# Transposing y by a copy through DRAM and by blocks on VectorE, in a kernel of 32 steps on one core

## The chip, the cores and the metric

The kernel runs on one core of a Trainium2 chip. The metric is device time in microseconds; the smaller, the better. All arithmetic that matters here is in float32. A core has a TensorE (matrix products, PE in the profile), a VectorE (DVE), a ScalarE (ACT), a GpSimd (POOL) and a SyncE (SP), which in this kernel issues most of the DMAs. Each engine works through its own instructions in order, and so does each queue of DMA issues; engines meet through semaphores.

## The reference

Two blocks follow each other, each with a residual sum and a layer norm behind it. The first is a layer that is trained on each token while it runs, the second a mixture of experts:

```python
def step(carry, kvq):                      # per sequence, 4096 tokens in order
    W, b = carry
    k, v, q = kvq                          # projections of the token, width 512
    pred = W @ k + b
    g = 2.0 / d_h * (pred - v)
    W = W - LR * jnp.outer(g, k)
    b = b - LR * g
    return (W, b), W @ q + b
...
x = layernorm(x + attn(x))                 # x: 2 sequences x 4096 tokens x 512
...
shared = silu(X @ sW1 + sb1) @ sW2 + sb2
logits = X @ routing_W + expert_bias       # 8 experts, the best 2 are used
activation = sqrt(softplus(logits))
routed = sum over the 2 best e of activation_e * (silu(X @ rW1_e + rb1_e) @ rW2_e + rb2_e)
x = layernorm(x + shared + routed)
```

The hidden width of each expert is 256.

## The kernel before

**Steps.** The 4096 tokens are cut into 32 chunks of 128, and one step of the loop, `step(c)`, treats chunk c of both sequences (B = 2). Inside a chunk the recurrence is solved as a triangular system. What a step needs of the inputs is made a step ahead: `prep(c + 1)` makes the keys and queries (tile KQ; PE tile pkq) and their products with each other (pa); `invert(c)` inverts the 32x32 blocks on the diagonal on VectorE, by 46 short instructions (line 375, tile X). Their result goes to DRAM and back (dX, CT; lines 382 and 384) and is then masked (C, D, DT, M; lines 388 to 397) for `join(c)`, which makes the inverse of the whole block (pn, pz). `step(c)` makes the residual R (pr, with theta_V and W; line 442), the output (po), the solved errors (pe) and the update of W (pw; line 494). The bias of W is kept up by an all-reduce on GpSimd (line 483) and two additions (line 485), followed there by x+brep (line 443).

**The second block, one step later.** `shared(c - 1)`, run in step c, takes the normalized y of the chunk before. It transposes y on TensorE into the tile pt (line 607), ScalarE copies pt to yT (line 609), and yT is then the stationary operand of the first product (ph, line 621), which gives the hidden layer of the shared expert and the router's logits. `router` picks two experts for each token, counts places (pq) and scatters the token's code into a table (gt, line 588; the index ri, line 585). y itself goes to DRAM (gy, line 613), y plus the second bias (line 630) plus the shared expert's output (py) too (gb, line 673).

**Experts.** Chunks 0 to 22 are one group, 23 to 30 another. When a group is complete, `routed` gathers its tokens expert by expert, and `collect` adds the two expert rows of each token to gb, takes the mean and the variance and writes the normalized rows. For group 0 the routed part runs in steps 24 to 27, collecting from step 28 on. Chunk 31 goes through all eight experts in `dense`, at the end, beside the collecting of group 1. `collect` finishes two chunks at a time (`finish`: one square root on ScalarE for both, then the scaling and the write).

**Order.** The order of TensorE and VectorE is written out: each part of a step is a generator that emits instructions and yields an amount, and `interleave` always continues the part of which the smallest share has been done. The share is the amount yielded so far over the total that the caller names for the part: 44 for a step, 13.5 for `prep`, 95 for `invert` and 13.5 for `shared`. The other engines and queues (ScalarE, GpSimd, SP) are ordered by the scheduler. A step's order on TensorE and VectorE follows from these numbers alone.

**A transpose without TensorE is already there, for K.** In steps 1 to 23 the keys are transposed in two moves. `exchange` writes the tile to DRAM in four DMAs (dT, line 304), one for each group of 32 columns, and reads it back in four others (G, line 307), so that quarters of partitions and quarters of columns change places; `turn_blocks` then transposes all 32x32 blocks in a single instruction of VectorE (line 315). The exchange of K is issued at the end of `prep(c + 1)`; its block transpose stands in the middle of the next step.

Of the kernel before, what the change touches and what calls it, by code (L numbers as in the profile page):

```python
# [41 lines left out]
F32 = mybir.dt.float32  # L42
BF16 = mybir.dt.bfloat16
I32 = mybir.dt.int32
AF = mybir.ActivationFunctionType
ALU = mybir.AluOpType
# [8 lines left out]
K = 2  # L55
# [5 lines left out]

SUMS = 23

TURNED = range(1, 24)
PSUM = bass.MemoryType.PSUM


# [39 lines left out]
def postln_block(ctx: ExitStack, tc: tile.TileContext, x, xT, thK, thV, thQ, w0, b0, masks, blk,  # L107
# [209 lines left out]
                                                                      a=NB, z=SB))  # L317


    prepared, turned = {}, {}  # L320

    def prep(c):
# [189 lines left out]
    def router(c, lg):  # L512
        def small(tag, shape=(P, B, E), bufs=1):
            return sm.tile(list(shape), F32, tag=tag, name=f"{tag}_{c}", bufs=bufs)


        u = small("u")
        nc.vector.scalar_tensor_tensor(u, lg, -1.0, lg, ALU.mult, ALU.min)
        nc.scalar.activation(u, u, AF.Exp)
        yield  # L520
        w = small("w")
        nc.vector.tensor_scalar(w, u, 1.0, None, ALU.add)
        lnw = small("lnw")
        nc.scalar.activation(lnw, w, AF.Ln)

        rank = small("rank")
        full = [P, B, E, E]
        other = lg[:, :, None, :].broadcast_to(full)
        own = lg[:, :, :, None].broadcast_to(full)
        gt = small("gt", full)  # L530
        nc.vector.tensor_tensor(gt, other, own, ALU.is_gt)
        eq = small("eq", full)
        nc.vector.tensor_tensor(eq, other, own, ALU.is_equal)
        nc.vector.tensor_tensor(eq, eq, lower[:, None].broadcast_to(full), ALU.mult)
        nc.vector.tensor_tensor(gt, gt, eq, ALU.add)
        nc.vector.tensor_reduce(rank, gt, AX.X, ALU.add)
        yield
        wm = small("wm")
        nc.vector.tensor_scalar(wm, w, -1.0, None, ALU.add)
        z = small("z")  # L540
        nc.vector.tensor_scalar(z, wm, 0.0, None, ALU.is_equal)
        nc.vector.tensor_tensor(lnw, lnw, z, ALU.add)
        nc.vector.tensor_tensor(wm, wm, z, ALU.add)
        nc.vector.reciprocal(wm, wm)
        nc.vector.tensor_tensor(lnw, lnw, wm, ALU.mult)
        nc.vector.tensor_tensor(lnw, lnw, u, ALU.mult)
        act = small("act")
        nc.vector.scalar_tensor_tensor(act, lg, 0.0, lnw, ALU.max, ALU.add)
        nc.scalar.activation(act, act, AF.Sqrt)
        if c not in of_step:  # L550

            nc.vector.scalar_tensor_tensor(act, rank, K - 0.5, act, ALU.is_lt, ALU.mult)
            yield act
            return

        gr = of_step[c]
        j = c - gr.c0
        chosen = sm.tile([P, B, E], BF16, tag="chosen", name=f"chosen_{c}")
        nc.vector.tensor_scalar(chosen, rank, K - 0.5, None, ALU.is_lt)
        sel = small("sel", (P, B, K, E))  # L560
        full = [P, B, K, E]
        nc.vector.tensor_tensor(sel, rank[:, :, None, :].broadcast_to(full),
                                kk[:, None, :, :].broadcast_to(full), ALU.is_equal)
        yield

        ps = ps_f.tile([P, 2, B, E], F32, tag="pf", name=f"pq_{c}")
        for s in range(B):
            nc.tensor.matmul(ps[:, 0, s], before, chosen[:, s], start=True, stop=(s == 0))
            for r in range(s):
                nc.tensor.matmul(ps[:, 0, s], ones16, chosen[:, r], start=False,  # L570
                                 stop=(r == s - 1))
        for s in range(B):
            nc.tensor.matmul(ps[:, 1, 0], ones16, chosen[:, s], start=(s == 0),
                             stop=(s == B - 1))
        yield
        place = small("place")
        nc.vector.tensor_tensor(place, ps[:, 0],
                                gr.next[:, None, :].broadcast_to([P, B, E]), ALU.add)
        nc.vector.tensor_tensor(gr.next, ps[:, 1, 0], gr.next, ALU.add)
        for what, to in ((place, gr.row), (act, gr.cw)):  # L580
            v = small("selv", (P, B, K, E))
            nc.vector.tensor_tensor(v, sel, what[:, :, None, :].broadcast_to(full), ALU.mult)
            nc.vector.tensor_reduce(to[:, j], v, AX.X, ALU.add)
        ri = sm.tile([P, B, K], I32, tag="ri", name=f"ri_{c}")
        nc.vector.tensor_copy(ri, gr.row[:, j])  # L585
        for s in range(B):
            for k in range(K):
                nc.gpsimd.indirect_dma_start(  # L588
                    out=gr.tables[s * K + k],
                    out_offset=bass.IndirectOffsetOnAxis(ap=ri[:, s, k:k + 1], axis=0),  # L590
                    in_=code[:, j * B + s:j * B + s + 1], in_offset=None,
                    bounds_check=E * gr.cap - 1, oob_is_err=False)

    def shared(c):
# [4 lines left out]
        y, norm = normed.pop(c)  # L599
        next(norm)  # L600
        yield 1.0
        yT = ytp.tile([P, DC, B, P], F32, tag="yT", name=f"yT_{c}")
        for dc in range(0, DC, 2):
            ps = ps_f.tile([P, 2, B, P], F32, tag="pf", name=f"pt_{c}_{dc}")
            for s in range(B):
                for i in range(2):
                    nc.tensor.transpose(ps[:, i, s, :], y[:, s, (dc + i) * P:(dc + i + 1) * P],
                                        ident)
            nc.scalar.copy(yT[:, dc:dc + 2].rearrange("p i s t -> p (i s t)"),
                           ps.rearrange("p i s t -> p (i s t)"))  # L610
        if gr:
            rows = slice((c - gr.c0) * T, (c - gr.c0 + 1) * T)
            nc.sync.dma_start(out=gr.y[rows].rearrange("(s p) d -> p s d", p=P), in_=y)
        yield 0.7

        lg = sm.tile([P, B, E], F32, tag="lg", name=f"lg_{c}")
        pre = hp.tile([P, B, HF + E], F32, tag="h", name=f"pre_{c}")
        for s in range(B):
            ps = ps_f.tile([P, HF + E], F32, tag="pf", name=f"ph_{c}_{s}")
            for dc in range(DC):  # L620
                nc.tensor.matmul(ps, yT[:, dc, s, :], w1_sb[:, dc, :],  # L621
                                 start=(dc == 0), stop=(dc == DC - 1))
            nc.scalar.copy(pre[:, s, :], ps)
            yield 1.5
# [68 lines left out]
    def dense(c):  # L693
# [4 lines left out]
        for e in range(E + 1):  # L698
            if e < E:
# [2 lines left out]
                    h = stepp.tile([P, 2, HC, T], F32, tag=("R", "K")[e // 2 % 2], name=f"hd_{e}", bufs=1)  # L702
                h_e[e] = h[:, e % 2]
                for hc in range(HC):
                    ps = ps_f.tile([P, T], F32, tag="pf", name=f"pd_{e}_{hc}")
                    for dc in range(DC):
                        nc.tensor.matmul(ps, w[:, dc * HF + hc * P:dc * HF + (hc + 1) * P],
                                         yT[:, dc].rearrange("p s t -> p (s t)"),
                                         start=(dc == 0), stop=(dc == DC - 1))
                    nc.scalar.activation(h_e[e][:, hc, :], ps, AF.Silu,  # L710
                                         bias=b1e_sb[:, e, hc:hc + 1])
                    yield 2.0
            if e > 0:
# [166 lines left out]
                weights(k + NW)  # L880
            yield 2.0

    squares, finish_at = [True], [(2, 3)]

    def collect(gr):

# [22 lines left out]
                    z.append(t)  # L909
                    yield  # L910

        def finish(parts, mean, var, on_scalar):

            if on_scalar:
                nc.vector.tensor_scalar(var, var, 1.0 / D, EPS, ALU.mult, ALU.add)
# [7 lines left out]
            for p, (c, acc) in enumerate(parts):  # L923
                for s in range(B):
                    m, v = mean[:, p, s:s + 1], var[:, p, s:s + 1]
                    if on_scalar:
                        nc.scalar.activation(acc[:, s, :], acc[:, s, :], AF.Identity,
                                             bias=m, scale=v)
                    else:
                        nc.vector.tensor_scalar(acc[:, s, :], acc[:, s, :], m, v,  # L930
                                                ALU.subtract, ALU.mult)
                nc.scalar.dma_start(out=out[:, c * P:(c + 1) * P, :].rearrange("s p d -> p s d"),
                                    in_=acc)
                yield

        for _ in fetch(0):
            pass
        yield 2.0
        done = iter(())
        for j in range(gr.n):  # L940
            c = gr.c0 + j
            ahead = fetch(j + 1)
            acc, z = got.pop(j)
            p = j % 2
            if p == 0:
                on_scalar, parts = squares[0], []
                two = sm.tile([P, 2, 2, B], F32, tag="fmv", name=f"fmv_{c}")
            mv = two[:, :, p]
            mean, var = mv[:, 0], mv[:, 1]
# [17 lines left out]
            else:  # L967
                for s in range(B):
                    st = sm.tile([P, 6], F32, tag="fst", name=f"fst_{c}_{s}")
                    nc.vector.bn_stats(st, acc[:, s, :])  # L970
                    nc.vector.bn_aggr(mv[:, :, s], st)
            if p == 1 or j == gr.n - 1:
                for _ in done:
                    pass
                done = finish(parts, two[:, 0, 0:p + 1], two[:, 1, 0:p + 1], on_scalar)
            yield 0.4
        for _ in done:
            pass
# [13 lines left out]
    for c in range(NCH):  # L992
# [3 lines left out]
        if c > 0:  # L996
            parts.append((INVERT, invert(c)))
        if c > 0:
            amount = SHARED + (PLAN if c in (b.c0, NCH - 1) else 0.0)
            parts.append((amount * (2 if c == NCH - 1 else 1), shared(c - 1)))  # L1000
        if c in spread:
            amount = (a.tiles + 3) * TILE / len(spread)
# [8 lines left out]
        if c == NCH - 2:  # L1011
            dense_weights(2)
    dense_weights(1 + B + 2)
    squares[0], finish_at[0] = False, (1, 3)
    interleave([(b.tiles * TILE, tiles[1]), (60.0, shared(NCH - 1)),
                ((a.n - sum(COLLECTED.values())) * COLLECT, collects[0])])
    squares[0] = True
    dense_weights(E - len(dense_w))
    interleave([(DENSE, dense(NCH - 1)), (b.n * COLLECT, collects[1])])


def _masks(np):
# [66 lines left out]
```

## Time and profile before

| What | Value |
|---|---|
| Median of 3 runs | 2638.32 us (2638.26 to 2647.33) |
| The profiled execution, its own time | 2633.89 us |
| Its span, first to last instruction | 2632.1 us |
| Mean granted TensorE clock | 0.989 |
| Length of each of the steps 1 to 22 | 58.66 us |
| VectorE idle before C (line 388), waiting for CT | 133.1 us in 27 waits |
| SP's dX waiting for the last instruction on X (line 382) | 364.6 us in 28 waits |
| Copies pt to yT on ScalarE | 64 of 128x512, 608 ns each |
| dT writes of K on SP | 92, median 680 ns of issue each, 128 KB |
| G reads of K on SP | 92, median 433 ns of issue each, 128 KB |

The span is cut into engines' busy times; an engine's idle time is put down to what ended it. The names are those of the tiles: `pt<-ident,x` is an instruction that writes the tile pt and reads ident and x (y lives in the tile x). The counts of matmul records are two for each float32 matmul of the program: `x8` at pkq is four matmuls, except for transposes, where eight records are eight transposes. Lines of SP's queue show the issue of a DMA, not its transfer.

### The profile page before, as it was taken

The numbers are of one execution on the slowest core, as the hardware profiler recorded it, in microseconds if no ns is written. First come the engines' busy times: TensorE is split into PE (matmuls) and PEld (weight loads), VectorE is DVE, ScalarE is ACT, GpSimd is POOL, SyncE is SP. The second block draws the span as 40 slices with busy tenths as digits, with TensorE's granted clock in tenths as the row PEclk, the third lists the DMA queues.
The fourth block names the chain that finished last, engine by engine and source line by source line (L and its number), as shares of the span: only waits on it lengthen the run. The fifth ranks groups of instructions, "written<-read, shape, count | busy, mean of one in ns | idle before, by whom it ended". The sixth has DMA issues, their size and how long they took to land.

```text
span 2632.1 us, 30914 instructions
## 1 busy us (share of the span) xinstructions
PE 2541.5 (97%) x10289; PEld 1642.1 (62%) x10289; DVE 1363.9 (52%) x3993; ACT 723.8 (27%) x1453; POOL 935.0 (36%) x796
## 2 busy tenths in 40 slices
PE   8999999999999999999999999999999999889897
PEld 6666666666666666666665676666767655446664
DVE  2566665565666655666666224223242466553345
ACT  1222222222222222222221232322323233334236
POOL 0223232223232322232324333333333334446654
PEclk9999999999999999999999999999999999989998
DMA  5122222222222222222223343353433456667777
GB/s 185 48 80 59 74 58 66 69 58 58 67 71 74 58 64 71 58 58 63 76 80 130 123 96 105 122 141 109 113 109 109 113 126 169 186 208 224 268 237 245
DMA packets 257647, 291.36 MB, mean 111 GB/s; under 512 B 158269, under 2 KB 171805, under 8 KB 253905
## 3 DMA queue, kind: packets, MB, share of 16 engines
q1 hardware_dynamic: 200624, 165.72, 22.1%
q0 software_dynamic: 48432, 107.42, 14.5%
q10 hardware_dynamic: 8432, 16.25, 1.6%
q8 instruction: 82, 1.34, 0.2%
q14 instruction: 77, 0.62, 0.1%
HBM read 344.38 MB, written 99.65 MB: 169 GB/s over the span
## 4 chain that ended last, share of the span: by engine, by line
PE 85%; issue 5%; DMA 4%; DVE 3%; POOL 2%; ACT 1%; SPq 0%; POOLq 0%; ACTq 0%; DVEq 0%
PE pkq L330 16%; PE pye L857 8%; PE po L449 8%; PE pr L433 8%; PE pr L438 8%; PE phe L846 8%; PE pw L493 8%; PE ph L621 4%; PE py L661 4%; PE pa L343 4%; PE pe L475 2%; PE po L487 2%; PE pg L837 2%; PE pz L414 2%; DMA wb<-wcat_in,widx 1%
## 5 line engine op out<-in xcount | busy, mean ns | idle before, releaser
L375 DVE SCALAR_TENSOR_TENSOR X<-L,X 128x31 f32<-128x31 f32 (+22 forms) x1472 | 409.0, 327 | 27.5 <-DMA L<-dL 10.5
L846 PEld LDWEIGHTS phe<-gT,wb 128*128 128x128 f32 x2208 | 269.7, 194 | 61.9 <-issue 58.9
L588 POOL DMA_INDIRECT gt<-code,ri x124 | 127.3, 1027 | 504.0 <-DVE ri L585 475.4
L860 DVE TENSOR_TENSOR o<-pye,wb 128x512 f32<-128x512 f32 x138 | 95.4, 692 | 400.8 <-PE pye L857 390.0
L857 PE MATMUL pye<-wb,he 128*128 128x512 f32 x552 | 268.7, 609 | 18.8 <-ACT he L850 11.9
L846 PE MATMUL phe<-gT,wb 128*128 128x128 f32 x2208 | 272.9, 277 | 7.0 <-DMA wb<-wcat_in,widx 5.6
L493 PE MATMUL pw<-R,K 128*128 128x512 f32 x496 | 240.6, 608 | 12.7 <-DVE x L488 7.9
L330 PE MATMUL pkq<-xT,thK 128*128 128x256 f32 x1024 | 242.8, 381 | 7.2 <-DMA thK<-thK_in 7.2
L828 POOL DMA_INDIRECT wb<-wcat_in,widx x138 | 144.8, 1049 | 286.2 <-DVE o L860 158.4
L330 PE MATMUL pkq<-xT,thQ 128*128 128x256 f32 x1024 | 244.9, 383 | 1.0 <-DVE Z L416 1.0
L330 PEld LDWEIGHTS pkq<-xT,thK 128*128 128x128 f32 x1024 | 195.0, 191 | 80.1 <-issue 59.3
L449 PE MATMUL po<-W,kq 128*128 128x512 f32 x512 | 242.6, 596 | 1.0 <-DVE K L471 1.0
L433 PE MATMUL pr<-thV,xT 128*128 128x512 f32 x512 | 240.7, 593 | 0.0
L438 PE MATMUL pr<-W,kq 128*128 128x512 f32 x512 | 240.2, 592 | 0.0
L330 PEld LDWEIGHTS pkq<-xT,thQ 128*128 128x128 f32 x1024 | 190.2, 191 | 46.9 <-issue 24.9
L483 POOL PARTITION_ALL_REDUCE ar<-R x23 | 141.6, 6158 | 206.4 <-issue 186.7
L850 ACT ACTIVATE he<-phe,wb 128x128 f32<-128x128 f32 x276 | 86.6, 364 | 436.5 <-PE phe L846 376.9
L337 ACT COPY kq<-pkq 128x256 f32<-128x256 f32 x256 | 82.8, 375 | 433.2 <-PE pkq L330 433.2
L494 DVE TENSOR_TENSOR W<-pw,W 128x512 f32<-128x512 f32 x248 | 168.5, 689 | 63.3 <-PE pw L493 59.6
L822 POOL DMA_INDIRECT g<-gy,gidx x138 | 139.8, 1013 | 153.4 <-PE pg L837 120.7
L493 PEld LDWEIGHTS pw<-R,K 128*128 128x128 f32 x496 | 91.4, 192 | 136.3 <-issue 97.8
L857 PEld LDWEIGHTS pye<-wb,he 128*128 128x128 f32 x552 | 98.5, 190 | 124.8 <-issue 90.8
(214 smaller groups left out, 3394.9 us busy)
## 6 DMA issues: line engine op xcount, KB each, us to landing
ge<-o SPq DMA_DIRECT2D x138, 256.0 KB
xT<-xT_in SPq DMA_DIRECT2D x32, 512.0 KB
x<-x_in SPq DMA_DIRECT2D x32, 512.0 KB
L<-dL SPq DMA_DIRECT2D x128, 128.0 KB
gy<-x SPq DMA_DIRECT2D x31, 512.0 KB
gb<-x SPq DMA_DIRECT2D x29, 512.0 KB
y_out<-acc ACTq DMA_DIRECT2D x29, 512.0 KB
dT_K<-kq SPq DMA_DIRECT2D x92, 128.0 KB
```

The costliest lines, as they stand in the source:

```text
L330: nc.tensor.matmul(ps[:, i].rearrange("p s t -> p (s t)"), th[:, dc, (ec + i) * P:(ec + i + 1) * P], xt[:, dc].rearrange("p s t -> p (s t) ...
L375: nc.vector.scalar_tensor_tensor(X[:, h, j + 1:], L[:, j + 1:, j], X[:, h, j:j + 1], X[:, h, j + 1:], ALU.mult, ALU.add)
L433: nc.tensor.matmul(ps, xt[:, dc, s, :], nthV_sb[:, dc, :], start=(dc == 0), stop=False)
L438: nc.tensor.matmul(ps, KQ[:, ec, s, 0, :], W[s][:, ec, :], start=False, stop=(ec == DC - 1))
L449: nc.tensor.matmul(ps, KQ[:, ec, s, 1, :], W[s][:, ec, :], start=(ec == 0), stop=False)
L483: nc.gpsimd.partition_all_reduce(ar, R, P, bass_isa.ReduceOp.add)
L493: nc.tensor.matmul(ps, K[s][:, ec, :], F[s], start=True, stop=True)
L494: nc.vector.tensor_tensor(W[s][:, ec, :], ps, W[s][:, ec, :], ALU.add)
L822: nc.gpsimd.indirect_dma_start(out=g_t[k], out_offset=None, in_=gr.y, in_offset=bass.IndirectOffsetOnAxis(ap=gr.gidx[:, k:k + 1], axis=0), ...
L828: nc.gpsimd.indirect_dma_start(out=wbuf[k % NW], out_offset=None, in_=wcat, in_offset=bass.IndirectOffsetOnAxis(ap=gr.widx[:, k:k + 1], ax ...
L846: nc.tensor.matmul(ps[:, hc, :], w[:, dc * HF + hc * P:dc * HF + (hc + 1) * P], t[:, dc, :], start=(dc == 0), stop=(dc == DC - 1))
L857: nc.tensor.matmul(ps, h[:, hc, :], w[:, O2 + hc * D:O2 + (hc + 1) * D], start=(hc == 0), stop=(hc == HC - 1))
```

## The change

In `shared(c)` for c = 1 to 21, which run in steps 2 to 22, the eight transposes on TensorE and the two copies on ScalarE are left out. y goes through `exchange` right after its write to gy is issued, then the generator yields `HELD` = 2.0, and `turn_blocks` writes yT. The total of `shared` grows by the same 2.0 in these steps, from 13.5 to 15.5. The tile yT has another layout, [P, B, DC, P] in place of [P, DC, B, P], in all steps, with the readers (ph, pd) and the copies that are left adapted to it. The copied tile G takes its buffer from the tag acc, which has four.

The instruction that makes `chosen` in `router` moves ahead by some ten instructions. In `collect` a chunk is finished alone where `paired[0]` is false (the part of group 0 that is collected in steps 28 to 31) and where it is one of a group's last two; else in pairs as before. For the last chunk of all, one sequence is scaled on VectorE and written through SP's queue, the other on ScalarE as before. The total that `interleave` is told for the collecting of group 1 is 1.1 times what it was.

```diff
@@ shared(c)
-        yT = ytp.tile([P, DC, B, P], F32, tag="yT", name=f"yT_{c}")
-        for dc in range(0, DC, 2):
-            ps = ps_f.tile([P, 2, B, P], F32, tag="pf", name=f"pt_{c}_{dc}")
-            for s in range(B):
-                for i in range(2):
-                    nc.tensor.transpose(ps[:, i, s, :], y[:, s, (dc + i) * P:(dc + i + 1) * P],
-                                        ident)
-            nc.scalar.copy(yT[:, dc:dc + 2].rearrange("p i s t -> p (i s t)"),
-                           ps.rearrange("p i s t -> p (i s t)"))
+        yT = ytp.tile([P, B, DC, P], F32, tag="yT", name=f"yT_{c}")
         if gr:
             rows = slice((c - gr.c0) * T, (c - gr.c0 + 1) * T)
             nc.sync.dma_start(out=gr.y[rows].rearrange("(s p) d -> p s d", p=P), in_=y)
+        if c in YTURNED:
+            g = exchange(y.rearrange("p s (c f) -> p (s c) f", f=P), f"y{c}")
+            yield HELD
+            turn_blocks(yT.rearrange("p s c t -> p (s c) t"), g)
+        for dc in range(0, DC, 2):
+            if c in YTURNED:
+                continue
+            ps = ps_f.tile([P, B, 2, P], F32, tag="pf", name=f"pt_{c}_{dc}")
...
         yield 0.7
@@ the readers of yT
-                nc.tensor.matmul(ps, yT[:, dc, s, :], w1_sb[:, dc, :],
+                nc.tensor.matmul(ps, yT[:, s, dc, :], w1_sb[:, dc, :],
...
-                                         yT[:, dc].rearrange("p s t -> p (s t)"),
+                                         yT[:, :, dc, :],
@@ collect
-            if p == 1 or j == gr.n - 1:
+            if p == 1 or not paired[0] or j >= gr.n - 2:
                 for _ in done:
                     pass
-                done = finish(parts, two[:, 0, 0:p + 1], two[:, 1, 0:p + 1], on_scalar)
+                done = finish(parts, two[:, 0, 0:p + 1], two[:, 1, 0:p + 1], on_scalar,
+                              gr is groups[-1] and j == gr.n - 1)
+                parts = []
@@ finish
-                    if on_scalar:
+                    if final and s == 0:
+
+                        nc.vector.tensor_scalar(acc[:, s, :], acc[:, s, :], v, m,
+                                                ALU.mult, ALU.add)
+                        nc.sync.dma_start(out=out[s, c * P:(c + 1) * P, :], in_=acc[:, s, :])
+                    elif on_scalar:
@@ the loop over steps and the end
-            amount = SHARED + (PLAN if c in (b.c0, NCH - 1) else 0.0)
+            amount = SHARED + (HELD if c - 1 in YTURNED else 0.0) + (PLAN if c in (b.c0, NCH - 1) else 0.0)
...
-    interleave([(DENSE, dense(NCH - 1)), (b.n * COLLECT, collects[1])])
+    interleave([(DENSE, dense(NCH - 1)), (1.1 * b.n * COLLECT, collects[1])])
```

with `HELD = 2.0` and `YTURNED = range(1, 22)`.

More of the change, by code (lines that the diff above doesn't have):

```diff
@@ L62 @@
 SUMS = 23
-TURNED = range(1, 24)
+TURNED, HELD = range(1, 24), 2.0
 PSUM = bass.MemoryType.PSUM
@@ L317, in turn_blocks @@
                                                                       a=NB, z=SB))
+    YTURNED = range(1, 22)
     prepared, turned = {}, {}
@@ L536, in router @@
         nc.vector.tensor_reduce(rank, gt, AX.X, ALU.add)
+        if c in of_step:
+            chosen = sm.tile([P, B, E], BF16, tag="chosen", name=f"chosen_{c}")
+            nc.vector.tensor_scalar(chosen, rank, K - 0.5, None, ALU.is_lt)
         yield
@@ L557, in router @@
         j = c - gr.c0
-        chosen = sm.tile([P, B, E], BF16, tag="chosen", name=f"chosen_{c}")
-        nc.vector.tensor_scalar(chosen, rank, K - 0.5, None, ALU.is_lt)
         sel = small("sel", (P, B, K, E))
@@ L613, in shared @@
             nc.sync.dma_start(out=gr.y[rows].rearrange("(s p) d -> p s d", p=P), in_=y)
+        if c in YTURNED:
[6 more added lines that the diff above has]
+            ps = ps_f.tile([P, B, 2, P], F32, tag="pf", name=f"pt_{c}_{dc}")
+            for s in range(B):
+                for i in range(2):
+                    nc.tensor.transpose(ps[:, s, i, :], y[:, s, (dc + i) * P:(dc + i + 1) * P],
+                                        ident)
+            nc.scalar.copy(yT[:, :, dc:dc + 2], ps)
         yield 0.7
@@ L704, in dense @@
                 for hc in range(HC):
-                    ps = ps_f.tile([P, T], F32, tag="pf", name=f"pd_{e}_{hc}")
+                    ps = ps_f.tile([P, B, P], F32, tag="pf", name=f"pd_{e}_{hc}")
                     for dc in range(DC):
                         nc.tensor.matmul(ps, w[:, dc * HF + hc * P:dc * HF + (hc + 1) * P],
-                                         yT[:, dc].rearrange("p s t -> p (s t)"),
+                                         yT[:, :, dc, :],
                                          start=(dc == 0), stop=(dc == DC - 1))
-                    nc.scalar.activation(h_e[e][:, hc, :], ps, AF.Silu,
+                    nc.scalar.activation(h_e[e][:, hc, :], ps.rearrange("p s t -> p (s t)"), AF.Silu,
                                          bias=b1e_sb[:, e, hc:hc + 1])
@@ L881, in routed @@
             yield 2.0
-    squares, finish_at = [True], [(2, 3)]
+    squares, finish_at, paired = [True], [(2, 3)], [False]
     def collect(gr):
@@ L910, in fetch, with finish @@
                     yield
-        def finish(parts, mean, var, on_scalar):
+        def finish(parts, mean, var, on_scalar, final):
             if on_scalar:
@@ L931, in finish @@
                                                 ALU.subtract, ALU.mult)
-                nc.scalar.dma_start(out=out[:, c * P:(c + 1) * P, :].rearrange("s p d -> p s d"),
-                                    in_=acc)
+                if final:
+                    nc.scalar.dma_start(out=out[1, c * P:(c + 1) * P, :], in_=acc[:, 1, :])
+                else:
+                    nc.scalar.dma_start(
+                        out=out[:, c * P:(c + 1) * P, :].rearrange("s p d -> p s d"), in_=acc)
                 yield
@@ L938, in collect @@
         yield 2.0
-        done = iter(())
+        done, parts = iter(()), []
         for j in range(gr.n):
@@ L943, in collect @@
             acc, z = got.pop(j)
-            p = j % 2
+            p = 0 if len(parts) != 1 else 1
             if p == 0:
-                on_scalar, parts = squares[0], []
+                on_scalar = squares[0]
                 two = sm.tile([P, 2, 2, B], F32, tag="fmv", name=f"fmv_{c}")
@@ L1013, in postln_block @@
     dense_weights(1 + B + 2)
-    squares[0], finish_at[0] = False, (1, 3)
+    squares[0], finish_at[0], paired[0] = False, (1, 3), True
     interleave([(b.tiles * TILE, tiles[1]), (60.0, shared(NCH - 1)),
```

## The prediction

> **What bounds it now.** I read the page's busy shares and its 40 slices, then one step of the loop engine by engine, because shares alone hide what waits inside a step.
>
> ```profile
> PE 2541.5 (97%) x10289; PEld 1642.1 (62%) x10289; DVE 1363.9 (52%) x3993; ACT 723.8 (27%) x1453; POOL 935.0 (36%) x796
> ```
>
> TensorE is busy nearly throughout. The step that begins at 843.92 us (c = 14), in the view by windows, is stricter: busy time equals length.
>
> ```profile
> 843.92:902.58 58.66, 58.66 (x210) 36.61 (x209) 35.14 (x108) 13.93 (x26) 17.61 (x13) 1.00 0.26 65
> ```
>
> Columns: window and length, then busy PE, PEld, DVE, ACT, POOL; clock, DMA share, GB/s. All of steps 1 to 22 last 58.66 us. So in the steps that the change touches each us off TensorE's order counts in full, and each us of wait put into it counts in full too. VectorE has 23 us to spare, but where? The timeline of VectorE at the head of the step:
>
> ```profile
> 848.41 7.18 DVE L375 SCALAR_TENSOR_TENSOR X<-L,X 128x29 f32<-128x29 f32 x36
> 857.16 0.69 DVE L442 TENSOR_TENSOR R<-pr,brep 128x512 f32<-128x512 f32 x1 [1.58 <-POOL brep L485]
> 857.77 5.87 DVE L375 SCALAR_TENSOR_TENSOR X<-L,X 128x4 f32<-128x4 f32 x8
> 868.26 0.24 DVE L388 STREAM_TRANSPOSE C<-CT 128x64 f32<-128x64 f32 x1 [4.62 <-DMA CT<-dX]
> ```
>
> The inversion's chain (L375) keeps VectorE until 863.64, 19.7 us into the step; over steps 2 to 22 this end lies at 19.2 to 21.0. The head of the step has no spare VectorE.
>
> **What is removed.** TensorE's timeline:
>
> ```profile
> 850.80 1.04 PE L607 MATMUL pt<-ident,x 128*128 128x128 f32 x8
> 851.68 1.88 PE L438 MATMUL pr<-W,kq 128*128 128x512 f32 x4
> 853.40 1.94 PE L621 MATMUL ph<-w,yT 128*128 128x264 f32 x8
> ```
>
> The eight transposes take 850.80 to 851.68, 0.88 us (their single times of 0.27 overlap). Over 21 steps: 18.5 us. [...] Two ScalarE copies (1.09 us a step) go too; ScalarE is 76% idle in the step: 0.
>
> **What is added: the place.** TensorE and VectorE follow the order in which `interleave` emits, lowest share first. In the new `shared` the exchange comes at 1.0/15.5, the block transpose at 3.0/15.5 = 0.194 and the first ph at 3.7/15.5 = 0.239 of the step (before: 1.7/13.5 = 0.126). The X chain is emitted until 23 x 0.7/95 = 0.169, the instructions on C at 26.1/95 = 0.275. So the transpose stands on VectorE **behind the whole X chain**, ahead of C. Before ph TensorE then has the pieces of `step` at 0, 2, 4, 6, 8.5 and 10.5 of 44 and of `prep` at 0 to 3 of 13.5: ten groups of 1.72 us. TensorE reaches ph at **17.2 us**.
>
> Its price is the one of K's:
>
> ```profile
> L315 DVE STREAM_TRANSPOSE K<-G_K 128x1024 f32<-128x1024 f32 x23 | 28.5, 1237 | 0.0
> ```
>
> 1.24 us. With the chain ending at 19.2 at best, ph can't start before 20.4: **at least 3.2 us of wait** where 0.88 was saved, even if the copy is free.
>
> **POOL moves the chain's end.** Emission of the router's pq and of place also slips: ri follows Z3 now (43.0 us, 15.7 before the step's end); in the new order it follows the pa evictions (about 45.0 of 57.8, 12.8 before the end, estimated by adding up the pieces). Behind ri POOL has four gt scatters, the all-reduce, brep, x+brep and y+b, in order, so these may come 2.8 us later in the next step. L442 waits for brep. [...] So the end is 20.1 (mean now) to 22.9; I take 21.5.
>
> **The copy, and SP's queue.** SP's timeline in this step:
>
> ```profile
> 848.51 0.38 SPq L613 DMA_DIRECT2D gy<-x  x1
> 848.99 0.42 SPq L150 DMA_DIRECT2D x<-x_in  x1
> 863.71 1.73 SPq L382 DMA_DIRECT2D dX<-X  x4
> 866.62 0.34 SPq L384 DMA_DIRECT2D CT<-dX  x1
> 867.00 2.75 SPq L304 DMA_DIRECT2D dT_K<-kq  x4
> 869.79 0.67 SPq L146 DMA_DIRECT2D xT<-xT_in  x1
> 870.51 0.44 SPq L307 DMA_DIRECT2D G_K<-dT_K  x1
> 892.61 1.73 SPq L354 DMA_DIRECT2D dL<-A  x4
> 894.39 0.43 SPq L307 DMA_DIRECT2D G_K<-dT_K  x1
> ```
>
> The y writes (2.75 us for four, as dT_K) go behind gy at about 5 us; the reads could go at about 8 and land by 13, well before the chain's end. They would cost nothing. But SP's order is the scheduler's, and it is in order: dX waits for the chain's last instruction, and all behind it with it. K's reads show where the scheduler puts a read: the first behind xT, the second behind dL, some 26 us after its write, the last two behind L. The first read shows by starting at once at 870.51 that data were there; the others were not held by data but by their places. The y writes have the same shape (128x8x32, four quarters). A place 20 us or more behind a write at 5 is behind dX, CT, dT_K and xT. I take that. From the chain's end: 6.9 us to the place where G_K stands (863.64 to 870.51), four reads of 0.44 = 1.8, then about 3 us to land: CT took 1.6 from issue to use with 32 KB, gy 4.0 with 512 KB in the chain of waits, and dT_K and xT lie ahead of the reads. Sum 11.7; with the transpose 12.9. At 21.5: ph at 34.4, **a wait of 17.2 us**, net 17.2 - 0.9 = 16.3 a step, x 21 = 343 us. Ends 20.1 and 22.9 for the chain: 314 and 372.
>
> Behind the waiting transpose stand C, D, DT, M and the second R. pn needs M; TensorE has 12.2 us from ph to pn, more than these 2 us, so nothing adds. SP's other work: x_in starts 2.7 us later, used two steps on; K's other reads 1.8 later, used half a step on. y+b on POOL must now await the y writes too; these land by 13, it starts at 15.2 or later in steps 2 to 22. The extra 1 MB a step adds to a DMA share of 0.26.
>
> **The rest.** `chosen` moves earlier: 0. yT's layout: the stationary blocks of ph stay contiguous; pd in the last stage reads two runs of 128: 0, at worst its 64 matmuls lengthen a little, which I don't price above 3 us. Single finishes in steps 28 to 31: seven more small sets (0.2 us ScalarE, three of 0.17 on VectorE) beside a full TensorE: 0. At the end the last tile no longer shares with its neighbour: from 2625.17 ScalarE does four scalings of 0.80; then one on ScalarE beside one on VectorE: 2 us less, and up to 3 more through the earlier order of collecting. I take -3.
>
> Sum: the profiled execution took 2633.9 us around its span of 2632.1; + 343 - 3 = 2974. The median of the runs is 4.4 higher; I say **2975**.
>
> **Rivals.**
> - *Reads early* (ahead of dX). For: SP idles from 849.4 to 863.7. Against: K's reads. Then ph starts at chain + 1.3: 21.4 to 24.2, wait 4.2 to 7.0, net 3.3 to 6.1: +70 to +128, about 2735. Chance 0.18.
> - *Reads between* (behind CT, ahead of dT_K): chain + 3.4 + 1.8 + 1.8 + 1.2 = 8.2; wait 11.1 to 13.9, net 10.2 to 13.0, about 2875. Chance 0.10.
> - *Faster*: the transpose ends before TensorE reaches ph. Its point: the chain must end by 15.9. Then 18.5 + 3 come off: 2612. For it: L375 alone at 232 ns x 46 is 10.7 us, so without POOL's adds it could be near. Against: 19.2 is the lowest of 21 steps. Chance 0.05.
> - *A draw*: waits of about the saving, 0.03.
> - *Main*: 0.62; 0.02 for slower in yet another way.
>
> A measurement here tells about 0.5% (13 us) from no change. Faster 0.05, same 0.03, slower 0.92. Main's own range is 2945 to 3010; I reach down to 2700 for the reads-early case.
>
> **What would show it.** Step length near 75 us in place of 58.66; TensorE idle before L621 (ph), released by the transpose; VectorE's transpose waiting on DMA of G_y; SP's reads behind xT. If instead the transpose follows the chain at once and the step is 62 to 65, it is reads-early. If TensorE shows no idle before ph, I am wrong altogether.

## The result and the profile after

The changed kernel took 2819.6 us (median of 4 runs, 2818.03 to 2822.7) against 2638.29 us: ratio 1.0699, 95% interval 1.0684 to 1.0714, **7% slower**. Its profiled execution took 2820.77 us around a span of 2819.0, which is 186.9 longer than before's.

The first part of its page:

```profile
PE 2584.3 (92%) x10121; PEld 1657.7 (59%) x10121; DVE 1432.0 (51%) x4036; ACT 703.5 (25%) x1424; POOL 933.3 (33%) x796
```

There are 168 matmuls fewer on TensorE than before, exactly the 21 x 8 transposes, and yet its busy time rose by 43 us and its share fell to 92%. Both need a reason. The step with c = 14 again, in the view by windows (length, then busy PE, PEld, DVE, ACT, POOL, clock, DMA share, GB/s):

```profile
941.59:1006.62 65.03, 59.90 (x202) 36.90 (x201) 39.11 (x109) 12.84 (x24) 17.68 (x12) 0.97 0.35 69
```

65.03 in place of 58.66, of which TensorE stands still for 5.1, and a clock of 0.97 where it was 1.00. TensorE's timeline in this step says where:

```profile
957.08 1.88 PE L434 MATMUL pr<-thV,xT 128*128 128x512 f32 x4
963.68 3.73 PE L628 MATMUL ph<-w,yT 128*128 128x264 f32 x8 [4.72 <-DVE yT L315]
967.25 1.88 PE L439 MATMUL pr<-W,kq 128*128 128x512 f32 x4
```

TensorE is done with pr 17.2 us into the step (957.08 + 1.72 - 941.59; a group of pr takes 1.72) and then waits for VectorE's block transpose. Once ph runs, its eight records last 3.73 where the second half of the same tile takes 1.94. VectorE's timeline:

```profile
947.74 10.38 DVE L376 SCALAR_TENSOR_TENSOR X<-L,X 128x29 f32<-128x29 f32 x36
958.04 0.68 DVE L443 TENSOR_TENSOR R<-pr,brep 128x512 f32<-128x512 f32 x1
958.64 3.79 DVE L376 SCALAR_TENSOR_TENSOR X<-L,X 128x4 f32<-128x4 f32 x8
962.38 1.25 DVE L315 STREAM_TRANSPOSE yT<-G_y 128x1024 f32<-128x1024 f32 x1
968.89 0.25 DVE L389 STREAM_TRANSPOSE C<-CT 128x64 f32<-128x64 f32 x1 [5.26 <-DMA CT<-dX]
```

The transpose starts the moment the chain on X ends, with no wait of its own: the copy through DRAM is there in time. What it lacks is VectorE. SP's queue shows why the copy was early:

```profile
947.85 0.38 SPq L607 DMA_DIRECT2D gy<-x  x1
948.26 0.55 SPq L304 DMA_DIRECT2D dT_y<-x  x1
948.92 0.83 SPq L150 DMA_DIRECT2D x<-x_in  x1
949.79 3.80 SPq L304 DMA_DIRECT2D dT_y<-x  x3
953.68 2.66 SPq L307 DMA_DIRECT2D G_y<-dT_y  x4
962.49 1.71 SPq L383 DMA_DIRECT2D dX<-X  x4
```

All four reads stand straight behind the writes and ahead of dX. And from the list of waits of the whole execution (us in total, times, longest):

```profile
PE ph L628 <- DVE yT L315: 126.2, 21, 9.3
```

21 waits, one in each of the steps concerned, 6.0 us each.

Summed by stage (start of a step's first matmul to the next):

| Stage | before | after |
|---|---|---|
| Steps 2 to 22 | 1231.9 | 1404.0 |
| Start to step 2, and steps 23 to 30 | 1067.0 | 1067.3 |
| Step 31, routed part of group 1, `dense` | 316.2 | 336.8 |
| Last TensorE instruction to the end | 17.0 | 10.9 |
| Span | 2632.1 | 2819.0 |

So 172.1 of the 186.9 us lie in the 21 steps, 8.2 us each. The other 14.8 are the last two stretches together, +20.6 and -6.1 (and 0.3); what lengthened the first of them was not taken apart. The mean step divides so: ph starts at 23.4 in place of 17.2, **+6.2**; the transposes are gone, **-0.9**; from ph to the step's end it takes 43.5, where the same order without a wait takes 40.6 (57.8 - 17.2), **+2.9**. The last term is the one that no row of before showed.

In the view by windows, TensorE is busy for 1269.2 us of these 21 steps, in place of 1231.9, though 18.5 us of transposes are gone, and the mean clock there is 0.95 in place of 1.00. The share falls by the waits, the busy time rises by the clock.

### The profile page after: what moved, and what is told of

Its sections match the earlier page's. It is cut to its first block, busy times and chain, and to the rows that moved or that the text cites. A ratio compares the mean times of both kernels' runs of the same rounds, so it can differ in the third digit from the quotient of the medians.

```text
span 2819.0 us, 30905 instructions
## 1 busy us (share of the span) xinstructions
PE 2584.3 (92%) x10121; PEld 1657.7 (59%) x10121; DVE 1432.0 (51%) x4036; ACT 703.5 (25%) x1424; POOL 933.3 (33%) x796
## 5 line engine op out<-in xcount | busy, mean ns | idle before, releaser
L628 PE MATMUL ph<-w,yT 128*128 128x264 f32 x512 | 163.7, 475 | 126.4 <-DVE yT L315 126.2
L439 PE MATMUL pr<-W,kq 128*128 128x512 f32 x512 | 247.1, 614 | 0.0
L628 PEld LDWEIGHTS ph<-w,yT 128*128 128x128 f32 x512 | 118.1, 236 | 185.2 <-DVE yT L315 143.6
L331 PEld LDWEIGHTS pkq<-xT,thQ 128*128 128x128 f32 x1024 | 189.4, 190 | 38.4 <-issue 15.5
```

Source lines behind the costliest of these rows:

```text
L331: nc.tensor.matmul(ps[:, i].rearrange("p s t -> p (s t)"), th[:, dc, (ec + i) * P:(ec + i + 1) * P], xt[:, dc].rearrange("p s t -> p (s t) ...
L439: nc.tensor.matmul(ps, KQ[:, ec, s, 0, :], W[s][:, ec, :], start=False, stop=(ec == DC - 1))
L628: nc.tensor.matmul(ps, yT[:, s, dc, :], w1_sb[:, dc, :], start=(dc == 0), stop=(dc == DC - 1))
```

## The experiments

The theory after the result: TensorE waits for the block transpose behind the X chain; the chain's end itself slid, because the router's ri moved and GpSimd with it; and the wait costs more than its length, because TensorE runs slowly after it. The rivals: a chain end set by VectorE's own work, a ph made slow by what it reads, and a part of the loss that belongs to the collecting. The time in each row is measured beside runs of before on the same chip. Chips differ by up to 0.5% (before took 2633.41 to 2646.70): collect_alone to filler_before_ph ran on one, after_again to ph_later_collect on another, reads_behind_CT on a third.

| Kernel | us | before beside it | ratio, 95% interval | steps 2 to 22 | X chain's end | ph starts | ph to step's end |
|---|---|---|---|---|---|---|---|
| before | 2638.29 | | 1 | 1231.9 | 20.1 | 9.5 | 49.2 |
| changed | 2819.6 | 2638.29 | 1.0699 (1.0684 to 1.0714) | 1404.0 | 22.1 | 23.4 | 43.5 |
| collect_alone | 2647.29 | 2645.33 | 1.0005 (0.9994 to 1.0016) | 1231.9 | 20.1 | 9.5 | 49.2 |
| exchange_alone | 2811.56 | 2645.33 | 1.0627 (1.0610 to 1.0645) | 1394.6 | 21.8 | 23.1 | 43.3 |
| place_ahead_of_A | 2765.75 | 2645.33 | 1.0450 (1.0423 to 1.0477) | 1353.0 | 19.9 | 21.1 | 43.3 |
| filler_before_ph | 2777.26 | 2645.33 | 1.0494 (1.0475 to 1.0514) | 1360.1 | 21.9 | 23.1 | 41.7 |
| after_again | 2809.72 | 2633.41 | 1.0677 (1.0657 to 1.0697) | 1388.6 | 21.4 | 22.7 | 43.5 |
| exchange_again | 2802.03 | 2633.41 | 1.0640 (1.0624 to 1.0656) | 1394.6 | 21.6 | 22.9 | 43.5 |
| ph_later | 2618.9 | 2633.41 | 0.9948 (0.9934 to 0.9962) | 1213.6 | 20.0 | 24.1 | 33.7 |
| ph_later_collect | 2622.12 | 2633.41 | 0.9959 (0.9946 to 0.9971) | 1213.6 | 20.1 | 24.1 | 33.7 |
| reads_behind_CT | 2933.16 | 2646.7 | 1.1093 (1.1058 to 1.1128) | 1518.0 | 21.6 | 28.8 | 43.5 |

The last four columns come from the profiled execution of each kernel; the last three are means over steps 2 to 22, in us from the step's first matmul.

**The two halves of the change.** One kernel keeps the collecting and drops the exchange, another the reverse.

```diff
-    YTURNED = range(1, 22)
+    YTURNED = range(0)
```

> The changed kernel with no step of y transposed through DRAM (the range of steps is empty); the new layout of yT and the changes in collecting stay. Theory A, the prediction's term: the collecting saves a little at the end, about 2635 us, and steps 2 to 22 last 58.66. Theory B, read off the changed kernel's trace, where the stretch from the start of the last step to the end took 347.7 us in place of 333.2: the collecting costs some 14 us by itself, about 2653.

> The changed kernel with collecting as it was before. Theory A (the collecting saves 3): about 2823 us. Theory B (the collecting costs 14, and the 173 us of steps 2 to 22 come from y's way alone): about 2806. Steps 2 to 22 last 67 us on average in both.

Collecting alone is within noise of before, so neither -3 nor +14 is its worth: 1.3 us, between -1.6 and +4.2. The exchange alone has nearly all of the loss, 166 us. The end does become shorter from the last TensorE instruction on (9.9 to 11.0 us with the new collecting in every run, 15.7 to 17.0 with the old one), but with the total unchanged, the stretch before it must have grown by about as much. Beside the exchange the collecting seemed to cost something (1.0699 against 1.0627 on two chips), so the two were measured side by side:

> The changed kernel unaltered, on the chip and beside the runs of the three others. All theories: a ratio to before near 1.070 as measured first.

> The changed kernel with collecting as before, once more, now on the same chip as the changed kernel. Theory A (collecting is worth nothing either way, as its run alone showed): within 0.3% of after_again. Theory B (collecting costs some 14 us when steps 2 to 22 are longer too): 0.5% below it.

1.0677 and 1.0640: 0.27% apart, just inside the 0.3% of theory A, but by 8 us and with intervals that almost touch. With ph_later below, the same pair differs by 3 us and the intervals overlap. Whether the new collecting costs a few us in some arrangements stays open; it wasn't taken apart further.

**Why the chain's end slid.**

```diff
         next(routing, None)
-        yield 0.5
+        yield 0.3 if c in YTURNED else 0.5
```

> The changed kernel with one yield of the router's tail cut from 0.5 to 0.3 in the steps concerned, so that place and ri stand ahead of the first eviction of pa on VectorE again. Theory A: the end of the chain on X slid by 2 us because ri, the scatters, the all-reduce and brep come 2.65 us later; with ri back near 15.5 us before the step's end, the chain ends near 20.1, the wait before ph shrinks by about 2 us a step, and the time falls by some 40 us to about 2780. Theory B: the chain's end is set by VectorE's own work and the wait stays: within 8 us of 2820.

The 0.2 decide whether place is emitted ahead of the first pa eviction or behind it. VectorE's timeline of step 14 of this kernel around ri:

```profile
956.31 0.42 DVE L417 TENSOR_TENSOR Z<-pz,DT 128x256 f32<-128x256 f32 x1 [1.40 <-PE pz L415]
956.65 0.17 DVE L579 TENSOR_TENSOR place<-pq,next 128x16 f32<-128x16 f32 x1
...
957.84 0.17 DVE L587 CAST ri<-row 128x4 int32<-128x4 f32 x1
...
961.39 0.29 DVE L347 TENSOR_SCALAR A<-pa 128x128 f32<-128x128 f32 x1 [0.98 <-PE pa L344]
```

place follows Z at once, and ri ends 16.3 us ahead of the next step on average, against 12.8 in the changed kernel and 15.5 before. The chain then ends at 19.9, as early as before, ph starts 2.3 us earlier, and steps 2 to 22 are 51 us shorter than in the changed kernel, 42 shorter than in exchange_alone on the same chip. Theory A holds: an instruction of 0.17 us, moved behind another engine's matmul, pushed four scatters and the all-reduce on GpSimd, and those the next step's chain. The rest of the wait, 21.1 - 17.2, remains.

Where the all-reduce meets the chain shows in means over steps 2 to 22 (starts and ends in us from the step's first matmul). Line 294 is the normalization of x, two instructions of VectorE at the head of the chain:

| | before | place_ahead_of_A | changed |
|---|---|---|---|
| All-reduce starts on GpSimd | -1.6 | -2.8 | 0.9 |
| Both normalizations take together | 2.05 | 1.60 | 3.95 |
| X chain starts | 3.6 | 3.4 | 5.4 |
| X chain lasts | 16.5 | 16.5 | 16.7 |
| Instructions of the chain beside GpSimd's additions | 7.5 | 8.1 | 7.5 |
| X chain ends | 20.1 | 19.9 | 22.1 |

The chain starts later; it hardly gets longer, and no more of it runs beside the additions. Of the 2.1 us, 1.9 are the normalizations. In step 14, before and in the changed kernel:

```profile
841.86 6.35 POOL L483 PARTITION_ALL_REDUCE ar<-R  x1 [8.07 <-issue]
846.40 0.55 DVE L294 TENSOR_SCALAR x<-x,amv,ars 128x512 f32<-128x512 f32 x1
```

```profile
941.41 6.13 POOL L484 PARTITION_ALL_REDUCE ar<-R  x1 [7.31 <-issue]
944.08 2.15 DVE L294 TENSOR_SCALAR x<-x,amv,ars 128x512 f32<-128x512 f32 x1
```

By itself such an instruction takes 0.55 us. In the changed kernel the first of the two always starts 2.49 us into the step and ends 4.81 us after the all-reduce began, in 19 of the 21 steps, so that it lasts up to 4.7. What holds it up inside the all-reduce, no run shows.

**Why it takes longer after the wait.**

```diff
+        if c in YTURNED:
+            ps = ps_f.tile([P, D], F32, tag="pf", name=f"pfill_{c}")
+            for _ in range(5):
+                nc.tensor.matmul(ps, ident, nthV_sb[:, 0, :], start=True, stop=True)
         lg = sm.tile(...)
```

> The changed kernel with five matmuls of 128x512 (4.3 us, result unread) on TensorE ahead of the first ph in the steps concerned, inside the wait. Theory A: the 3 us a step that neither the wait nor the order explain come from a TensorE clock that is halved after the idle stretch; filler keeps it up, ph's eight records take 1.9 us in place of 3.7, and the time falls by about 38 us to 2782. Theory B: ph runs slowly because of what it reads or of transfers beside it; then it stays at 3.7 and the time within 8 us of 2820, or more where the filler exceeds the wait.

TensorE's timeline in step 14 of this kernel:

```profile
924.53 1.88 PE L434 MATMUL pr<-thV,xT 128*128 128x512 f32 x4
926.25 4.45 PE L626 MATMUL pfill<-thV,ident 128*128 128x512 f32 x10
931.02 2.05 PE L632 MATMUL ph<-w,yT 128*128 128x264 f32 x8 [0.32 <-DVE yT L315]
```

ph starts where it did (23.1), since VectorE sets that, but runs in 2.05 in place of 3.73, and the time from ph to the step's end falls from 43.5 to 41.7. Adding 4.3 us of useless work a step brings the ratio down from the changed kernel's 1.0677 and 1.0699 to 1.0494, some 50 us across chips, and 34 us below exchange_alone on the same chip (38 were expected). The granted clock of this step is 1.00 again. The data read and the transfers are unchanged, so the slowness is TensorE's own, after an idle stretch. In step 14 of the changed kernel it shows as 4.7 us idle, then records 0.44 us apart in place of 0.22, for the 3.6 us from 963.68 to 967.25; the trace's clock stands at half there for 3.4 us, from 963.78 on. This step lost 1.8 us by it (3.73 in place of 1.94 for the eight records).

Over all steps it is more. The trace's clock stands at half in each of the 21 steps of the changed kernel, whose idle times are 4.0 to 9.3 us, for 3.4, 6.8 or 10.2 us, beginning in the idle time or shortly behind it. Half of what lies behind the start of ph comes to 2.3 us a step. Another 0.4 is a wait at pe for Z (9.1 us in 22 waits), which the new order made by putting pe straight behind the last pz. That leaves 0.2 of the 2.9. In filler_before_ph the same sum is 0.4 at half clock, the 0.4 at pe and 0.2: the 1.1 that its 41.7 lies above 40.6. The length of the idle time does not decide alone: five of the 21 steps of filler_before_ph still had a half-clock stretch, behind idle times of 2.3 to 3.5 us; two of place_ahead_of_A had none behind 3.6 and 3.8.

**What the place in SP's queue is worth.** The prediction's main branch put the reads of y behind dX, CT, dT_K and xT. They were not there, so the price of a late place was untested. This kernel moves them back, though not as far: in each of the 21 steps the first read stands ahead of dX, two behind dX and the last behind CT, where the rival reads between had it. The main branch's own place stays untested.

```diff
-            g = exchange(y.rearrange("p s (c f) -> p (s c) f", f=P), f"y{c}")
+            t = send(y.rearrange("p s (c f) -> p (s c) f", f=P), f"y{c}")
             yield HELD
+            g = fetch_back(t, f"y{c}")
             turn_blocks(yT.rearrange("p s c t -> p (s c) t"), g)
```

(`send` and `fetch_back` are the two halves of `exchange`.)

> The changed kernel with the four reads of y emitted just ahead of the block transpose in place of just behind the writes; in SP's order the first then stands ahead of dX, two behind dX and the last behind CT. Theory A (the place in SP's queue matters as the prediction reckoned it, only the place itself was read wrongly from K): the last read is issued some 3.8 us behind the X chain's end, lands about 2 us later, the transpose ends 7 us behind the chain in place of 1.2, and each of the 21 steps grows by some 5.8 us: about 120 us over the changed kernel, near 2930 beside a before of 2638. Theory B (the reads are needed no earlier, or VectorE's order hides them): within 15 us of the changed kernel.

SP's queue in step 14 of this kernel, then VectorE's timeline there:

```profile
952.61 1.74 SPq L387 DMA_DIRECT2D dX<-X  x4
954.39 0.90 SPq L308 DMA_DIRECT2D G_y<-dT_y  x2
955.47 0.34 SPq L389 DMA_DIRECT2D CT<-dX  x1
955.86 0.43 SPq L308 DMA_DIRECT2D G_y<-dT_y  x1
```

```profile
947.65 4.88 DVE L380 SCALAR_TENSOR_TENSOR X<-L,X 128x4 f32<-128x4 f32 x8
958.38 1.25 DVE L319 STREAM_TRANSPOSE yT<-G_y 128x1024 f32<-128x1024 f32 x1 [5.84 <-DMA G_y<-dT_y]
```

Now the transpose does wait for its data, 5.84 us, and ends 7.1 behind the chain in the mean. The kernel takes 2933 us. The same four DMAs with the same bytes, further back in a queue that stands still for the X chain, cost another 114 us (steps 2 to 22: 1518.0 in place of 1404.0; about 120 were expected).

**A version that takes the gain.** If the wait and what follows from it are all, the saving must appear once ph stands where VectorE has had time, and ri where it was. The collecting is the old one here, and the new one in ph_later_collect.

```diff
-            yield HELD
+            yield 3.0
...
-        yield 0.7
+        late = c in YTURNED
+        yield 2.5 if late else 0.7
...
-            yield 1.5
+            yield ((0.15, 1.05)[s] if late else 1.5)
...
-        yield 0.7 if c < NCH - 5 else 2.5
+        yield 0.6 if late else (0.7 if c < NCH - 5 else 2.5)
         next(routing, None)
-        yield 0.5
+        yield 0.3 if late else 0.5
...
-            yield 3.0
+            yield 4.0 if late else 3.0
```

The paces of pht and of the next one go from 0.7 to 0.5, and the total of `shared` grows by 3.95 in place of 2.0.

> Collecting as before; y by the copy and blocks as in the changed kernel, but the paces of shared are set so that ph stands behind the second pair of pr with W and a further pkq (TensorE would reach it at 24.1 us of the step in place of 17.2), and pht, pq, place close up behind it, so that ri is ahead of the first pa eviction again; the block transpose stays behind the X chain and ahead of C. Theory A (the loss is the wait behind the X chain, plus the slowed clock after it, and nothing else): the chain ends near 20, the transpose at 21.3, ph finds its data, steps 2 to 22 last 57.8 us, and the kernel is 18.5 us faster than before, ratio 0.993. Theory B (C now 1.2 us later on VectorE and CT later behind dT_K on SP make pn wait, or the router's packed chain does): steps of 58.5 to 60, ratio 0.999 to 1.01.

> ph_later with the changed kernel's collecting. Theory A (collecting is worth nothing): within 0.2% of ph_later. Theory B (it saves at the very end, some 5 us from the last TensorE instruction on): 0.2% below ph_later.

The step with c = 14 of ph_later by windows, and the head of ph and of the transpose in the timelines of TensorE and VectorE:

```profile
834.09:891.88 57.79, 57.79 (x202) 35.66 (x201) 38.81 (x109) 12.84 (x24) 17.35 (x13) 1.00 0.34 81
```

```profile
856.46 1.89 PE L331 MATMUL pkq<-xT,thQ 128*128 128x256 f32 x8
858.18 3.72 PE L629 MATMUL ph<-w,yT 128*128 128x264 f32 x16
```

```profile
854.57 1.25 DVE L315 STREAM_TRANSPOSE yT<-G_y 128x1024 f32<-128x1024 f32 x1
861.02 0.25 DVE L389 STREAM_TRANSPOSE C<-CT 128x64 f32<-128x64 f32 x1 [5.21 <-DMA CT<-dX]
```

TensorE is busy for the whole step again, without the 0.88 us; the transpose is ready at 855.8, 2.4 us ahead of ph. Steps 2 to 22 take 1213.6, 18.3 less than before, as the row of the eight transposes said (18.5). The kernel is faster than before by half a per cent, 0.9948 (0.9934 to 0.9962), about 14 us. Theory B (pn or the router made to wait) has no room: no step is longer than 57.79.

## Why the prediction was right, and where it wasn't

That the kernel would be slower, and by a wait of TensorE at ph behind the X chain, was forecast and came. The number is another matter. The main branch, 2975 with a chance of 0.62, did not come about. 2819.6 lies inside the stated 2700 to 3010 because these reached down for reads early, and it lies between the 2735 of that branch and 2975 because a term was missing that neither had. That is luck. Step by step:

- *Each us put into TensorE's order counts in full*: right. 21 x 8.2 is the loss.
- *0.88 us a step by the row of the eight transposes, 18.5 us in all*: right. ph_later got 18.3 us out of it.
- *The transpose stands behind the whole X chain, TensorE reaches ph at 17.2, at least 3.2 us of wait*: right in each number; ph waits in all 21 steps, the mean chain end is 22.1, the transpose takes 1.245.
- *POOL moves the chain's end, to between 20.1 and 22.9*: right in size. The 21.5 in the sum, 1.4 behind the mean of before, was the author's estimate, and no run shows the slide by way of brep that it rests on: VectorE's waits for brep at R are 12.5 us in 7 waits, against 13.4 in 7 before. What the runs show in its place: ri ends 12.8 us before the step's end, as reckoned, and the chain's end moved by 1.3 to 2.1 us in the six traces with the new order; place_ahead_of_A took it back. The path was another. The rival *Faster* has L375 slowed by GpSimd's additions. It is slower there (median 1.29 us beside them, 0.23 without), but as much before as after; the delay arises ahead of the chain, in the normalization beside the all-reduce (3.95 us for the two instructions in place of 2.05); why it is held up there, no run shows. The transpose kept its 1.245 us, with no GpSimd instruction beside it in any of the 21 steps.
- *"K's reads show where the scheduler puts a read"*: **this step failed.** It read a fixed distance of 20 us or more between write and read out of K's queue and carried it over to y, although in the same lines the first read of K stands only 0.8 us behind the last write (867.00 + 2.75 to 870.51). The reads of y stand directly behind their writes, in all of these steps. What differs in the program is that `exchange` of y is emitted ahead of dX, that of K behind dL and L; but why the scheduler spread K's reads isn't settled by these runs. The 12.9 us from the chain's end to ph that followed from it are 1.3 in the run. The branch reads early, given 0.18, is the one that came, and the main forecast of 2975 is 155 us too high (its last sum is 2978 with the 4.4 us that it names).
- *Price of reads early, +70 to +128*: too low, +181 came. The wait was inside its bounds (6.2 in 4.2 to 7.0). The missing term is the time after the wait, 2.9 us x 21 = 61 us, 2.3 of the 2.9 at half clock: a wait on TensorE was priced at its length alone. The same term (3.0 there) is missing in reads between: 2875 was said, and reads_behind_CT, which has its last read where that branch put it, took 2933.
- *-3 for collecting*: the last stretch did fall by 6 us, but the time before it grew by as much or more; alone it is 1.3 us, from -1.6 to +4.2.
- *SP, ScalarE, and the extra 1 MB a step at nothing*: right. The transpose follows the chain at once in each of the 21 steps, and ph_later has the same copies at no cost.

## What to carry to other kernels

Work that is moved to an engine with spare time in the mean must be looked up at its place in that engine's order: what stands ahead of it there, and when the receiver comes to ask for it. The same exchange was 7% slower or 0.4% faster (ph_later_collect), by nothing but the paces of the parts around it. In this kernel stalls of 3.3 to 13.4 us on TensorE cost their length and then 2.1 to 2.3 us more at half clock, in the means of six traces.

## What was not expected of the hardware

- In step 14 of the changed kernel, after 4.7 us of idle, TensorE ran at half its pace for 3.6 us (records of 128x264 0.44 us apart in place of 0.22), and five unread matmuls in the gap made the kernel about 1.8% faster relative to before (1.0494 against 1.0677 to 1.0699).
- VectorE's normalization of 128x512, 0.55 us by itself, took up to 4.7 beside GpSimd's all-reduce, and ended 4.81 us after the all-reduce began in 19 of 21 steps.
- Eight float32 transposes of 128x128 in a row take 0.11 us each on TensorE, though single records last 0.27.
- The four writes of y in pieces of 128 bytes and the four reads take about 8 us of SP's time from the first issue to the last (948.26 to 956.34), with half a MB each way, and nothing on the other engines showed it in ph_later.
